# Adding the gated shift to x with an accumulating DMA instead of GpSimd additions

## The chip, the cores and the metric

The kernel runs on one core of a Trainium2 chip. The metric is the device time of one execution in microseconds. The kernel before took 761.77 us, the median of three runs (760.84 to 761.86). A profiled execution took 761.13 us; its span, from the first to the last recorded instruction, is 759.3 us. A core has five engines with queues of their own: TensorE (PE, matmuls), VectorE (DVE), ScalarE (ACT), GpSimd (POOL) and SyncE (SP, which here only issues DMAs). ACT and POOL can issue DMAs too.

## The reference

One transformer block with adaptive layer norms, on x of shape (8, 1024, 256) in float32; the eight batches are independent. Per batch there are six modulation rows sa, ca, ga, sb, cb, gb of 256 elements.

```python
h = _layernorm(x) * (1 + ca) + sa
x = x + ga * _L0_attn_ref(h, L0_attn_w_lhs, L0_attn_w_rhs)   # softmax((h*wl)(h*wr)^T) @ h
h = _layernorm(x) * (1 + cb) + sb
x = x + gb * _L0_ffn_ref(h, L0_ffn_W1, L0_ffn_b1, L0_ffn_W2, L0_ffn_b2)
```

The attention's values are h itself. With xn the normalized x, h = xn * (1 + ca) + sa, and since each row of the softmax sums to one, ga * attention = softmax @ (xn * (1 + ca) * ga) + sa * ga. The kernel uses this: it multiplies xn by the row (1 + ca) * ga, and adds the row sa * ga, the gated shift, to x ahead of the attention. That second addition is what the change is about.

## The kernel before, in words

A batch is 8 tiles of 128 rows, in two halves of 4 tiles (`g` = 0 and 1). x of a half is one tile in SBUF, 128 partitions x 4 x 256, in a pool of six buffers; it is loaded by ACT's DMA queue (`load_x`), updated in place and stored by SP's queue (`y_out`).

The main loop runs over batches `b` and row tiles `i`, and overlaps three things: the attention of batch b, the MLP of batch b - 1 and the preparation of batch b + 1. PE computes scores (`direct`, L410), the products with the normalized x (`product`, L499, and `pair_begin`/`pair_end`, L547 and L591, which do the same for two tiles with fewer multiplications), and the MLP (`pair_products`, L724, and `y_first`/`y_second`, L804). The fewer multiplications cost additions: POOL makes sums of weight blocks, of the exponentials (`left_sum`, `left_sums`, L563 to L575), of the MLP's input (`ffn_turn`, `hs`, L712 to L715), of its hidden layer (`pair_last` L778, `pair_turn` L797 to L800) and of the normalized x (`right_sums`, L532), and it adds the MLP's output to x (`y_add`, L878).

Transposes are made in three steps: DVE turns blocks of 32 x 32, four DMAs on SP's queue write the result to DRAM (`D_a`, `D_m`, `D_f`, `D_y`; L304), and one reads it back in the other order (L307; `X_a`, `X_f`, `Y`, `sc`). For the MLP's input the chain is: the second norm on ACT (`ffn_norm`, X_f), DVE's turn, D_f, X_f, then `hT` on DVE and ACT (L703, L705), then `hs` on POOL, then PE's L724.

For a half of the next batch, DVE takes statistics, ACT normalizes (L279, `xg`), DVE turns `xg` (`T_a`), and then `x_plus` and `xg_times` add the shift row to x and multiply `xg` by its row. Both rows lie broadcast in an SBUF tile `rows`, loaded per batch from a DRAM tile `rows_d` (`load_rows`).

The order of every engine's instructions is that of the program text: the function `pin` fixes it. `x_plus` and `xg_times` don't issue where they are called. They append to a queue, four entries each (one per tile), and calls of `spare` take one entry at a time. For the first half the calls are at i = 2 and the entries issue at i = 2 and 3; for the second half the calls are at i = 4 and the entries issue at i = 6 and 7, since the tiles i = 4 and 5 call no `spare`. In the first half POOL's order is: hs of the earlier half, 4 `x_plus`, 4 `xg_times`, the left sums for the pair of tiles 3 and 4. In the second: the left sums of the pair 6 and 7, 4 `x_plus`, 3 `xg_times`, `hs`, the fourth `xg_times`, `right_sums`. A half of x with the shift added is next read when the attention's result is added to it, in the next batch (`product_out` L513, `pair_out` L619, on DVE).

Of the kernel before, what the change touches and what calls it, by code (L numbers as in the profile page):

```python
# [13 lines left out]
ALU = mybir.AluOpType  # L14
# [3 lines left out]
P = 128  # L18
# [6 lines left out]
def adaln_block_kernel(  # L25
# [13 lines left out]
    nc = tc.nc  # L39
    B, S, D = x.shape  # L40
# [5 lines left out]
    TH = HALF // P  # L46
# [35 lines left out]
    x_t = {}  # L82
# [19 lines left out]
    def load_x0(q, queue):  # L102
# [11 lines left out]
        out=wv[ND : 2 * ND, :], in_=w_rhs.rearrange("a b (k p) -> (a b k) p", p=P)  # L114
# [518 lines left out]
    queue = deque()  # L633
# [5 lines left out]
    def later(out, in0, row, op):  # L639
        queue.append(lambda: nc.gpsimd.tensor_tensor(out, in0, row, op))  # L640
# [25 lines left out]

    def x_plus(b, g):

        for t in range(g * TH, (g + 1) * TH):
            xr = x_tile(b, t)  # L670
            later(xr, xr, rows_t[b][:, 1, :], ALU.add)
# [308 lines left out]
    rows_d = dram.tile([B, 4, D], F32, name="rows_d")  # L980
# [76 lines left out]
    for g in range(2):  # L1057
        x_plus(0, g)
# [18 lines left out]
    def early(b, i):  # L1077

        if b == 0:

            if i in (1, 3):
                prepare_rstd(1, i // 2)
            elif i == 5:
                ffn_rstd(0, 0)
            if i in (2, 3):
                prepare_norm(1, i - 2)
                x_plus(1, i - 2)
            if i in (3, 4):
                xg_times(1, i - 3)
            elif i == 5:  # L1090
                prepare_turn(1, 0)
                sum_w2()
            elif i == 6:
                load_x(2, 0)
        else:
            if i == 2 and b + 1 < B:
                prepare_norm(b + 1, 0)
            elif i == 6 and b + 2 < B:
                load_x(b + 2, 0)
# [22 lines left out]
    def norms(b, i):  # L1122
        if b > 0 and i == 0:
            ffn_blocks(b - 1, 1)
        if b == 0:
            if i == 0:
                prepare_start(1)
                prepare_stats(1, 0)
            elif i == 1:
                prepare_stats(1, 1, range(TH // 2))  # L1130
                sum_w1()
            elif i == 2:
                prepare_stats(1, 1, range(TH // 2, TH))
        elif b + 1 < B:
            if i == 1:
                prepare_start(b + 1)
                prepare_stats(b + 1, 0)
            elif i == 2:
                prepare_blocks(b + 1, 0)
                x_plus(b + 1, 0)  # L1140
                xg_times(b + 1, 0)
        elif i == 5:

            ffn_blocks(b, 0)
        if b == B - 1:
            return
        if i == 6:
            if b == 0:
                ffn_norm(b, 0)
            ffn_blocks(b, 0)  # L1150
# [234 lines left out]
    b = B - 1  # L1385
# [74 lines left out]
```

## Time and profile before

| What | us | Share |
|---|---|---|
| Median of three runs | 761.77 | |
| Profiled execution | 761.13 | |
| Its span | 759.3 | |
| PE busy, 3876 matmuls | 750.9 | 99% |
| DVE busy | 576.0 | 76% |
| POOL busy, 658 instructions | 570.8 | 75% |
| ACT busy | 374.7 | 49% |
| POOL, `x<-x,rows`, 64 additions | 44.8 | 6% |
| DMA queues, busy share of 16 engines | | 38.5% (SP), 3.6% (ACT) |

Busy time of an engine is the sum of its recorded instructions. Matmuls are pipelined, so two of them overlap in the records and PE's share says only that there is hardly a moment without one. A wait line names the instruction that was late, what released it, the total, how often, and the longest. In a timeline a line has the start, the length, the engine, the line of the kernel, what it writes and reads, and in brackets the idle time before it with what ended that. "SPq" is SP's queue issuing a DMA: its length is the issuing alone. Packets of a DMA are recorded too, with their queue, size and time.

### The profile page before, as it was taken

The page shows a single profiled execution, that of the slowest core. Times are in us where ns is not written, and L with a number is a line of the kernel's source. Part 1 is how long each engine was busy: PE and PEld are TensorE (multiplying, and loading weights), DVE is VectorE, ACT ScalarE, POOL GpSimd, SP SyncE. Part 2 cuts the span into 40 slices and gives each one's busy share as a digit, 9 for nine tenths or more (in the row PEclk, how much of TensorE's full clock was granted, in tenths as well). Part 3 has the DMA queues.
Part 4 walks back from the last instruction along what each step waited for, and adds up shares of the span by engine and source line. Part 5 has one row for each costly group of instructions (what it writes and reads, how often), then busy time and mean ns, then how long its engine had stood idle before and what let it go on. Part 6 is the DMA issues. An engine that isn't in the chain of part 4 may idle for free.

```text
span 759.3 us, 11880 instructions
## 1 busy us (share of the span) xinstructions
PE 750.9 (99%) x3876; PEld 623.3 (82%) x3876; DVE 576.0 (76%) x1259; ACT 374.7 (49%) x688; POOL 570.8 (75%) x658
## 2 busy tenths in 40 slices
PE   8999999999999999999999999999999999999998
PEld 4676789888897889878888888988889788888887
DVE  6787788778797788968888787877889677685632
ACT  3454545635466363655537444563546635252521
POOL 3542988788968799687887799777996888669731
PEclk9999999999999999999999999999999999999999
DMA  5314442465433554535534545235553354134220
GB/s 196 126 56 132 119 133 73 129 187 170 129 98 110 180 148 126 144 106 160 164 89 138 152 151 156 80 116 176 157 155 76 115 177 137 45 91 125 82 85 28
DMA packets 106213, 95.21 MB, mean 125 GB/s; under 512 B 29700, under 2 KB 98848, under 8 KB 106152
## 3 DMA queue, kind: packets, MB, share of 16 engines
q1 hardware_dynamic: 98408, 85.81, 38.5%
q10 hardware_dynamic: 7744, 8.65, 3.6%
q8 instruction: 30, 0.49, 0.3%
q14 instruction: 31, 0.25, 0.1%
HBM read 50.62 MB, written 43.81 MB: 124 GB/s over the span
## 4 chain that ended last, share of the span: by engine, by line
PE 88%; DVE 4%; ACT 2%; DMA 2%; POOL 2%; issue 1%; SPq 0%; DVEq 0%
PE psc L410 15%; PE pa L724 10%; PE pr L591 7%; PE po L499 6%; PE pb L724 6%; PE yc L804 6%; PE pc L724 6%; PE ya L804 6%; PE yb L804 6%; PE pq L591 5%; PE pp L547 5%; PE py L914 4%; PE yd L804 3%; DMA X_a<-D_a 1%; PE pmr L192 1%
## 5 line engine op out<-in xcount | busy, mean ns | idle before, releaser
L410 PE MATMUL psc<-rT,lT 128*128 128x512 f32 (+3 forms) x384 | 135.2, 487 | 1.0 <-ACT rT L373 0.8
L778 POOL TENSOR_TENSOR f<-f,kept 128x512 f32<-128x512 f32 x64 | 81.5, 1274 | 40.4 <-DVE f L777 18.5
L417 ACT COPY sc<-psc 128x512 f32<-128x512 f32 (+3 forms) x96 | 44.8, 475 | 120.4 <-PE psc L410 113.1
L482 ACT ACTIVATE pT<-pT 128x1024 f32<-128x1024 f32 x64 | 67.6, 1056 | 66.8 <-DVE pT L473 66.8
L410 PEld LDWEIGHTS psc<-rT,lT 128*128 128x128 f32 x384 | 66.3, 191 | 38.7 <-issue 24.1
L473 DVE TENSOR_TENSOR pT<-sc,pm 128x1024 f32<-128x1024 f32 x64 | 77.4, 1209 | 25.7 <-PE pm L466 15.3
L499 PE MATMUL po<-xg,pT 128*128 128x257 f32 x352 | 80.7, 380 | 0.0
L461 DVE TENSOR_REDUCE m<-sc 128x1 f32<-128x1024 f32 x64 | 77.4, 1209 | 1.3 <-ACT sc L417 1.0
L499 PEld LDWEIGHTS po<-xg,pT 128*128 128x128 f32 x352 | 66.2, 190 | 10.0 <-issue 1.0
L745 ACT COPY kept<-pa 128x512 f32<-128x512 f32 x64 | 37.3, 583 | 68.6 <-PE pa L724 68.6
L724 PE MATMUL pb<-hs,w1s 128*128 128x256 f32 x256 | 65.9, 380 | 0.1
L724 PE MATMUL pc<-hT,w 128*128 128x256 f32 x256 | 65.7, 379 | 0.0
L640 POOL TENSOR_TENSOR x<-x,rows 128x256 f32<-128x256 f32 x64 | 44.8, 732 | 24.9 <-ACT xg L279 10.7
L787 ACT ACTIVATE f<-f 128x512 f32<-128x512 f32 x64 | 39.8, 622 | 35.9 <-POOL f L778 35.9
L878 POOL TENSOR_TENSOR x<-x,Y 128x512 f32<-128x512 f32 x28 | 35.1, 1276 | 29.4 <-DMA Y<-D_y 23.9
L724 PEld LDWEIGHTS pb<-hs,w1s 128*128 128x128 f32 x256 | 48.5, 190 | 7.3 <-DVE f L763 0.8
L724 PEld LDWEIGHTS pc<-hT,w 128*128 128x128 f32 x256 | 48.6, 190 | 6.7
L804 PE MATMUL yc<-f,w2s 128*128 128x256 f32 x224 | 51.3, 379 | 0.0
L433 DVE STREAM_TRANSPOSE Tm<-sc 128x896 f32<-128x896 f32 (+6 forms) x49 | 34.4, 702 | 19.9 <-ACT sc L417 19.1
L804 PEld LDWEIGHTS yc<-f,w2s 128*128 128x128 f32 x224 | 41.5, 190 | 8.1 <-issue 2.9
L797 POOL TENSOR_TENSOR ft<-f 128x256 f32<-128x256 f32 x56 | 40.9, 730 | 7.6 <-ACT f L788 7.5
L547 PEld LDWEIGHTS pp<-xg,pT 128*128 128x128 f32 x336 | 41.9, 192 | 5.1 <-issue 1.4
(164 smaller groups left out, 1823.3 us busy)
## 6 DMA issues: line engine op xcount, KB each, us to landing
D_f<-T_f SPq DMA_DIRECT2D x60, 128.0 KB, 2.4
X_f<-D_f SPq DMA_DIRECT2D x15, 512.0 KB, 3.9
D_a<-T_a SPq DMA_DIRECT2D x56, 128.0 KB, 3.4
D_y<-T_y SPq DMA_DIRECT2D x56, 128.0 KB, 2.7
Y<-D_y SPq DMA_DIRECT2D x14, 512.0 KB, 3.4
out_dram<-x SPq DMA_DIRECT2D x14, 512.0 KB, 4.2
X_a<-D_a SPq DMA_DIRECT2D x13, 512.0 KB, 3.4
x<-in_L_attn_x_dram ACTq DMA_DIRECT2D x12, 512.0 KB, 3.9
```

What stands on the lines that cost most here:

```text
L410: nc.tensor.matmul(psc[:, : hi - lo], lhsT=lT_t[b, i // TH][:, k, ts(i % TH, P)], rhs=rT_t[b, n][:, k, lo - n * HALF : HALF], start=(k == ...
L417: nc.scalar.copy(score_row(b, i)[:, lo // V : hi // V, :], psc[:, : hi - lo].rearrange("p (n v) -> p n v", v=V),)
L461: nc.vector.tensor_reduce(m, score_row(b, i), AX.XY, ALU.max)
L473: nc.vector.tensor_tensor(pT.rearrange("p j (a v) -> p j a v", v=V), score_columns(b, i), pm[:, :P].rearrange("p (j a v) -> p j a v", j=1, ...
L482: nc.scalar.activation(pT_t[b, i], pT_t[b, i], AF.Exp)
L499: nc.tensor.matmul(po[:, : D + 1], lhsT=pT[:, t, :], rhs=xg_t[b][:, t, 0 : D + 1], start=(t == 0), stop=(t == NT - 1),)
L547: nc.tensor.matmul(out, lhsT=lhs[:, t, :], rhs=xg_t[b][:, h * TH + t, P : P + XS], start=(t == 0), stop=(t == TH - 1),)
L591: nc.tensor.matmul(out, lhsT=lhs[:, t, :], rhs=rhs[:, t, :], start=(t == 0), stop=(t == TH - 1),)
L640: queue.append(lambda: nc.gpsimd.tensor_tensor(out, in0, row, op))
L724: nc.tensor.matmul(out, lhsT=lhsT, rhs=rhs, start=True, stop=True)
L778: nc.gpsimd.tensor_tensor(f[:, c::NH, hi], f[:, c::NH, hi], kept[:, None, hi].to_broadcast([P, 2, H2]), ALU.add,)
L804: nc.tensor.matmul(out, lhsT=lhs(c), rhs=rhs(c), start=(c == 0), stop=(c == NH - 1))
```

## The change

In batches 2 to 7 `x_plus` appends one entry instead of four. The entry issues a DMA from POOL's queue, which reads the shift row of `rows_d` in DRAM, broadcast to 128 partitions and 4 tiles, and adds it to x of the half where it lies (`accum_op`). Batches 0 and 1 keep POOL's additions. That makes 12 DMAs of 512 KB in place of 48 additions of 128 x 256. `xg_times` is as before, with its four entries.

```diff
     def x_plus(b, g):
 
+        if b > 1:
+            queue.append(lambda: nc.gpsimd.dma_start(
+                out=x_t[b, g],
+                in_=rows_d[b][1:2, :].partition_broadcast(P).to_broadcast([P, TH, D]),
+                accum_op=ALU.add,
+            ))
+            return
         for t in range(g * TH, (g + 1) * TH):
             xr = x_tile(b, t)
             later(xr, xr, rows_t[b][:, 1, :], ALU.add)
```

The instructions of PE, DVE, ACT and SP stay the same and in the same order. On POOL the DMA stands where the first of the four additions stood; since three entries are gone, the entries of `xg_times` are taken three calls earlier, and in the second half all four now come before `hs`. The instructions that read x next (L513 and L619 on DVE, L656 on ACT, the store on SP) get a wait for the DMA's landing; six waits of PE for POOL, in L499, go away.

## The prediction

> **What bounds the kernel now.** First the page: busy time by engine, then the chain that ended last.
>
> ```profile
> PE 750.9 (99%) x3876; PEld 623.3 (82%) x3876; DVE 576.0 (76%) x1259; ACT 374.7 (49%) x688; POOL 570.8 (75%) x658
> PE 88%; DVE 4%; ACT 2%; DMA 2%; POOL 2%; issue 1%; SPq 0%; DVEq 0%
> ```
>
> PE is busy 99% of the span and carries 88% of the chain; POOL, from which the change takes work, has 2%. Busy time of pipelined matmuls can hide stalls, so I looked for a rhythm: the chain in order of time has one run of 16 `yc` matmuls in the second half of each batch from the second on.
>
> ```profile
> 114.80 3.46 PE yc L804 x16
> ...
> 205.23 3.46 PE yc L804 x16
> ...
> 295.66 3.46 PE yc L804 x16
> ...
> 386.26 3.46 PE yc L804 x16
> ...
> 476.69 3.46 PE yc L804 x16
> ...
> 567.12 3.46 PE yc L804 x16
> ...
> 658.06 3.45 PE yc L804 x16
> ```
>
> The steps are 90.43, 90.43, 90.60, 90.43, 90.43 and 90.94 us. Four are equal to the hundredth: in these PE issues back to back. The other two lose 0.17 and 0.51 us. All 12 new DMAs lie between 114 and 620 us, so a lighter POOL can return at most 0.17 + 0.51 = 0.68 us, or 0.09%. The larger of the two (at 595 us) isn't POOL's: there the scores wait for ACT's `rT`, which waits for the landing of `X_a`. So the question is not what is gained but whether one of the twelve sites gets late enough to stop PE.
>
> The timeline of POOL in the third batch (b = 2), first half's additions:
>
> ```profile
> 203.03 2.84 POOL L640 TENSOR_TENSOR x<-x,rows 128x256 f32<-128x256 f32 x4
> 205.83 2.78 POOL L640 TENSOR_TENSOR xg<-xg,rows 128x256 f32<-128x256 f32 x4
> ...
> 216.70 1.27 POOL L778 TENSOR_TENSOR f<-f,kept 128x512 f32<-128x512 f32 x1 [2.82 <-DVE rs L275]
> ```
>
> Second half's additions, and what comes after them:
>
> ```profile
> 246.57 2.77 POOL L640 TENSOR_TENSOR x<-x,rows 128x256 f32<-128x256 f32 x4
> 249.31 2.11 POOL L640 TENSOR_TENSOR xg<-xg,rows 128x256 f32<-128x256 f32 x3
> 255.37 0.73 POOL L712 TENSOR_TENSOR hs<-hT 128x256 f32<-128x256 f32 x1 [3.95 <-DVE hT L703]
> ...
> 256.73 0.73 POOL L714 TENSOR_TENSOR hs<-hT,hs 128x256 f32<-128x256 f32 x1
> ```
>
> Both runs end in an idle time of POOL, 2.82 and 3.95 us, that waits for another engine: shortening the run lengthens the idle, and PE sees nothing. Then the DMA queue of SP, ACT and PE around the second site:
>
> ```profile
> 246.24 1.83 SPq L304 DMA_DIRECT2D D_f<-T_f  x4
> 250.49 0.34 SPq L307 DMA_DIRECT2D X_f<-D_f  x1
> ```
>
> ```profile
> 254.48 0.81 ACT L705 ACTIVATE hT<-X_f,modT 128x512 f32<-128x512 f32 x1 [0.37 <-DMA X_f<-D_f]
> ```
>
> ```profile
> 259.82 0.59 PE L724 MATMUL pa<-hs,w 128*128 128x256 f32 x2
> 260.25 1.03 PE L724 MATMUL pb<-hs,w1s 128*128 128x256 f32 x4
> ```
>
> The MLP's input is turned through DRAM just there: D_f, X_f, then `hT`, then `hs` on POOL, then PE. `hs[1]` (L714) ends at 257.46 and PE wants it at 260.25: 2.79 us of slack. In the six batches that issue the new DMA (b = 1 to 6) the same difference is 2.79, 2.79, 2.38, 2.30, 1.48 and 2.72.
>
> **What the skill says.** The Trainium skill, "DMA: Bandwidth & Descriptors", section "SWDGE vs HWDGE vs iDMA": accumulating in a DMA exists only for DMAs issued from GpSimd, where Q7 cores compute the descriptors in software. The kernel before issues none from POOL (its queues are `hardware_dynamic` and `instruction`), so the trace neither confirms nor prices this. "Perfetto Trace Analysis", section "DMA Instruction — SWDGE (GPSIMD)": cores 0 and 1 generate, and the recorded end is their last descriptor, not the landing; no run here shows it yet. "GPSIMD Engine Reference", section 3.1, gives about 2.6 cycles an element for a two-input add: 256 x 2.6 / 1.2 GHz = 555 ns plus dispatch, and the trace agrees with 732 ns for 256 columns.
>
> **The change part by part.** *Removed*: 48 of the 64 `x<-x,rows` additions (b = 2 to 7, 8 each): 48 x 0.732 = 35.1 us of POOL, 6% of its busy time. PE gets none of it, by the idles above: 0.
>
> *Added on POOL*: 12 DMA issues, one per half, each with 128 x 4 destination rows of 1 KB, so 512 writes, and two reads for each (the row of `rows_d` and the old x), 1024. Let X be how long POOL is held. Lower end 1 us: the DMA page's specification table has about 1 us to the first byte on this path. Upper end 14.2 us: its fit has a fixed 2.0 us for a DMA, and its 1 MiB example has 144 descriptors a side; were all 2.0 us generation, that is 13.9 ns each, times 1024. The page lays most of the 2.0 us on the receipt, and only 1.0 - 0.6 = 0.4 us apart from the hardware path: 2.8 ns each. My value is 1 + 1024 x 0.0028 = 3.9 us (an estimate).
>
> What X may be for nothing: at the first site, the 2.84 us removed plus the idle, which in the six batches is 2.29 to 2.82: 5.1 to 5.7 us. Beyond it `f+kept` (L778) is late, then ACT's relu (0.7 us of slack, 217.97 to 218.64), behind it on ACT an exponent and the copy `kept`, whose release PE awaits at 224.88 (copy ends 224.17): 0.7 us more. PE stops from about 7 us. The left sums (L563 to L575), queued behind the DMA too, end 7 us before PE's use (213.88 against 220.84). At the second site: 2.78 + idle (2.72 to 5.20) - 0.73 for the fourth `xg` multiplication, which now comes before `hs`, + the slack of `hs`: 7.5 to 9.5 us. With X = 3.9 both are covered: 0. Without the cover it would be 12 x (3.9 - 2.8) = 13 us.
>
> *Moved*: x_plus puts one entry in the queue instead of four, so `xg` comes three pops earlier and PE loses one wait on POOL per batch; the transposes that read `xg` before it is overwritten end at 200.3 for the first half and 220.1 for the second (DVE's timeline), before either site: 0. SP's and ACT's queues keep their order.
>
> *Added waits*: the next reader of x on DVE (L513, L619), ACT (L656) and SP's output now also wait for the landing. Issued at about 203, the half is first read by L513 after PE's `po` of 265.70, 62 us later, the second half still later; the slowest landing of 512 KB here is 6.8 us. Cost 0.
>
> *Added traffic*: the load of x, also 512 KB in packets of 1 KB (512 packets, 241.87 to 244.12 us), has a mean of 54 ns a packet: 32 packets on each of 16 engines, 1.7 us. "Collectives: The Full Stack", section "The bandwidth ceiling", says an accumulating copy needs two source reads and runs at half the rate of a copy: 108 ns, 3.5 us of every engine. Lower end 1.7 (only as costly as a copy); upper end 200 ns a packet, what the 4 KB packets of X_f take here, 6.4 us. At the first site the turn X_a <- D_a is beside it, whose reader on ACT comes at 219.68, 11 us after its landing: 0. At the second, D_f and X_f are beside it. They share the engines, so X_f lands later by about half to all of 3.5 us: 1.7 to 3.5. Against the slacks, 1.7 costs 0.2 (b = 5 alone), 3.0 costs 0.2+0.2+0.6+0.7+1.5+0.3 = 3.5, 4.0 costs 9.5 us. I take 2.0: 0.5 us in b = 5; less some 0.2 that POOL's relief may return at the two uneven steps.
>
> *Sum*: the profiled execution took 761.13 us, 759.3 span + 1.83 around it. 761.13 + 0.5 - 0.2 = 761.4. It stood 0.64 under the median 761.77, so against the median: about 762.0.
>
> **Rivals.** (1) *Issue too long*: POOL held over 7 us at the first sites. For it: software descriptors, 512 rows with two reads, and nothing in the trace to say they are cheap. Against it: the page's "small, variable". At X = 8: six first sites x 1 us plus about 1 = 7, so 769; at 10: 6 x 3 + 9 = 27, so 789. This is the slower side, and it decides at X about 7. (2) *Traffic*: X_f late beyond 2.5 us at the second site. For it: DMA share 0.63 in 246 to 252 us. Against it: D_f starts before the issue ends. At 3 to 4 us of lateness 765 to 771. (3) *The relief counts*: the 0.68 us come back whole, 761.1; 0.2% (1.5 us) would need stalls that the rhythm excludes. (4) *The addition leaves POOL in name only*: POOL is held until the data lands. A load of 512 KB lands 3.9 us after its issue; with 1.7 us more for the second read X is near 5.6, still under 7: 762 as well, with the two idles used up.
>
> **How the numbers follow.** Hidden (with 3 and 4): 0.58. Rival 1: 0.22. Rival 2: 0.15. Faster by more than 0.2%, from something unseen: 0.05. A fifth of a per cent, 1.5 us, is about what measurement tells (the runs spread over 1.0 us). So faster 0.05, same 0.58, slower 0.37. The likeliest case alone: 761.0 to 763.3. The range: 760.3 below (0.05 left out) and 775 above (X to about 8.7, lateness to 4.6; about 0.13 left out).
>
> **What would show it.** Right: `yc` still 90.4 us apart, PE's waits on POOL absent, POOL's busy time near 536 us with the idle before L778 and L712 there in part. Wrong: idle before L778 gone and ACT's relu waiting on POOL (rival 1); a longer wait of `hT` for X_f and PE idle at `pa` or `pb` (rival 2); DVE's L513 or L619 waiting for the accumulating DMA (landing price wrong).

## The result, and the profile after

The changed kernel takes 789.24 us (median of four runs, 787.4 to 791.13) against 761.46 us for the kernel before on the same chip: ratio 1.0364, 95% interval 1.034 to 1.0387. It is 28 us slower; 762.0 was forecast, in a range up to 775. The side was a rival's, the second one (traffic at the second site); its size was not foreseen.

The page of the changed kernel, busy time, DMA queues and chain:

```profile
PE 762.3 (97%) x3876; PEld 624.9 (80%) x3876; DVE 580.5 (74%) x1259; ACT 373.5 (48%) x688; POOL 553.6 (70%) x622
...
q1 hardware_dynamic: 98408, 85.81, 36.9%
q0 software_dynamic: 6336, 6.29, 7.6%
...
PE 69%; DMA 15%; DVE 5%; POOL 3%; ACT 3%; issue 2%; SPq 2%; DVEq 0%; POOLq 0%
```

POOL lost work as intended (the twelve issues, 1.3 us each, give back 15.6 of the 35.1 us removed). But DMA now carries 15% of the chain (2% before), and PE's busy time rose by 11 us with the same 3876 matmuls. The run of `yc` matmuls, 90.43 us apart before, now starts at 115.11, 209.90, 304.71, 398.62, 493.70, 591.03 and 684.61 us: steps of 94.79, 94.81, 93.91, 95.08, 97.33 and 93.58, together 26.2 us more than before. So the loss lies in the six batches that issue the DMAs. PE's own waits, largest three:

```profile
PE pa L731 <- DVE hT L710: 8.0, 6, 2.8
PE pb L731 <- POOL hs L721: 3.5, 6, 0.7
PE pa L731 <- ACT kept L752: 2.5, 3, 1.4
```

Six waits for `hT`, six for `hs`: one per batch, at the second site. The timeline there (third batch, lines of POOL, SP, ACT and PE picked out):

```profile
250.90 1.82 SPq L304 DMA_DIRECT2D D_f<-T_f  x4
...
251.60 1.30 POOL L670 DMA_DIRECT2D x<-rows_d  x1
...
256.13 0.34 SPq L307 DMA_DIRECT2D X_f<-D_f  x1
256.51 4.24 SPq L304 DMA_DIRECT2D D_m<-Tm  x4
...
264.79 0.81 ACT L712 ACTIVATE hT<-X_f,modT 128x512 f32<-128x512 f32 x1 [6.01 <-DMA X_f<-D_f]
...
265.33 0.70 PE L731 MATMUL pa<-hT,w 128*128 128x256 f32 x2 [1.12 <-DVE hT L710]
```

POOL is held 1.3 us and is not the problem. X_f is issued at 256.13 and `hT` starts at 264.79: 8.7 us, where the kernel before took 4.0 (250.49 to 254.48). The new DMA's own group:

```profile
L670 POOL DMA_DIRECT2D x<-rows_d x12: 1292/1298/1438, 113.3 to 634.2; - x12
...
DMA to landing us min/median/max: 9.5/10.5/11.7
```

It lands 10.5 us after its issue. The busy stretches of two microseconds have the DMA engines' share and GB/s at the end:

```profile
252.00:254.00 2.00, 2.00 (x12) 1.72 (x11) 1.23 (x2) 0.50 (x1) 2.00 (x4) 1.00 1.03 331
254.00:256.00 2.00, 2.00 (x11) 1.77 (x10) 2.00 (x2) 0.99 (x1) 1.71 (x3) 1.00 0.84 122
256.00:258.00 2.00, 2.00 (x15) 1.87 (x14) 1.60 (x5) 0.81 (x3) 0.00 (x0) 1.00 1.15 76
258.00:260.00 2.00, 2.00 (x20) 2.00 (x19) 1.42 (x2) 0.78 (x2) 0.00 (x0) 1.00 1.05 69
260.00:262.00 2.00, 2.00 (x18) 1.95 (x17) 0.00 (x0) 0.00 (x0) 0.00 (x0) 1.00 1.06 172
```

From 256 to 260 us the DMA engines are recorded as fully occupied (1.15 and 1.05) and move 69 to 76 GB/s, less than a quarter of the 331 a moment earlier. In the packet records these are 62 to 76 packets of 1 KB of the new queue per microsecond. No packet of SP's queue starts between 255.7 and 260.1: X_f, asked for at 256.13, hasn't begun. In the kernel before, its first packet starts 0.97 us after its issue; here it is 2.9 to 5.6 us in five of the six batches, after 260 to 375 packets of the new queue. So POOL is not late, and the bytes are few: one slow transfer is under way, and what is behind it waits.

In the remaining one (b = 5) it is D_f that is held:

```profile
536.61 3.44 SPq L304 DMA_DIRECT2D D_f<-T_f  x4
546.19 0.34 SPq L307 DMA_DIRECT2D X_f<-D_f  x1
```

X_f is issued 9.6 us after D_f, against 4.7 before. D_f had begun when the DMA's packets came, and it isn't stopped: from 540 to 543 us, 83 to 110 packets of the new queue pass per microsecond and 56 to 79 of D_f between them; in the third batch 323 of D_f passed in one microsecond (253 to 254), just ahead of the new queue's.

Of the 26.2 us, 6.8 are not waiting at all. After the stalls of the batches b = 1, 2 and 5 the granted TensorE clock is half for 3.4, 3.4 and 6.8 us; half of these 13.65 us is lost. In the same view, with PE's granted clock third from the end:

```profile
268.00:270.00 2.00, 2.00 (x6) 1.61 (x6) 1.89 (x6) 0.33 (x2) 1.92 (x3) 0.51 0.94 319
```

PE counts as busy there and does half the work, which is where most of its 11 us more of busy time come from. Without the clock, the first `pb` matmul of the six second sites starts 2.84, 2.59, 2.09, 2.78, 4.26 and 2.32 us later after the `yd` matmuls than before, 16.9 us in all; the wait for `kept` grew by 1.8. Together with the clock this is 25.5 of the 26.2 us.

### The profile page after: what moved, and what is told of

Read it like the earlier page. It is cut to its first block, busy times and chain, and to the rows that moved or that the text cites. A ratio compares the mean times of both kernels' runs of the same rounds, so it can differ in the third digit from the quotient of the medians.

```text
span 785.9 us, 11892 instructions
## 1 busy us (share of the span) xinstructions
PE 762.3 (97%) x3876; PEld 624.9 (80%) x3876; DVE 580.5 (74%) x1259; ACT 373.5 (48%) x688; POOL 553.6 (70%) x622
## 4 chain that ended last, share of the span: by engine, by line
PE 69%; DMA 15%; DVE 5%; POOL 3%; ACT 3%; issue 2%; SPq 2%; DVEq 0%; POOLq 0%
PE psc L410 10%; PE pa L731 9%; PE pb L731 6%; PE pc L731 6%; DMA X_f<-D_f 6%; PE po L499 6%; PE pr L591 5%; PE ya L811 4%; PE yb L811 4%; PE pp L547 4%; PE py L921 4%; PE yc L811 4%; PE pq L591 3%; DMA D_f<-T_f 3%; DMA D_m<-Tm 2%
## 5 line engine op out<-in xcount | busy, mean ns | idle before, releaser
L499 PE MATMUL po<-xg,pT 128*128 128x257 f32 x352 | 80.7, 380 | 0.0
L499 PEld LDWEIGHTS po<-xg,pT 128*128 128x128 f32 x352 | 66.2, 190 | 10.0 <-issue 1.0
L731 PE MATMUL pb<-hs,w1s 128*128 128x256 f32 x256 | 69.0, 393 | 3.6 <-POOL hs L721 3.5
L731 PE MATMUL pc<-hT,w 128*128 128x256 f32 x256 | 68.1, 390 | 0.0
L719 POOL TENSOR_TENSOR hs<-hT 128x256 f32<-128x256 f32 x16 | 11.6, 725 | 71.5 <-DVE hT L710 71.5
L885 POOL TENSOR_TENSOR x<-x,Y 128x512 f32<-128x512 f32 x28 | 35.1, 1275 | 35.7 <-DMA Y<-D_y 35.7
L731 PEld LDWEIGHTS pb<-hs,w1s 128*128 128x128 f32 x256 | 48.8, 195 | 14.1 <-POOL hs L721 6.2
L731 PEld LDWEIGHTS pc<-hT,w 128*128 128x128 f32 x256 | 50.2, 197 | 7.7 <-DVE pr L609 0.4
L731 PE MATMUL pa<-hT,w 128*128 128x256 f32 x128 | 39.0, 387 | 8.0 <-DVE hT L710 8.0
```

The source lines that it names most:

```text
L499: nc.tensor.matmul(po[:, : D + 1], lhsT=pT[:, t, :], rhs=xg_t[b][:, t, 0 : D + 1], start=(t == 0), stop=(t == NT - 1),)
L731: nc.tensor.matmul(out, lhsT=lhsT, rhs=rhs, start=True, stop=True)
```

## The experiments

All comparisons are with the kernel before on the same chip.

**Which site?** The DMA for one half only; the other half keeps POOL's additions.

```diff
-        if b > 1:
+        if b > 1 and g == 0:      # first half only; g == 1: second half only
```

> The accumulating DMA only for the first half of x (6 DMAs), POOL's additions for the second half. Theory (the MLP's turn is held up): all of the loss comes from the second half's DMA, which holds up the read of X_f beside it; without it the time is that of the kernel before, 761 to 762 us, and ACT's hT follows the issue of X_f by 4.0 us as before. Rival (any such DMA costs, through POOL's issue or through the clock): half of the loss stays, about 775 us.

> The DMA only for the second half. Theory: the whole loss is here, 786 to 790 us, hT 8.7 to 9.6 us after the issue of X_f. Rival (any such DMA costs): about 775 us.

First half only: 763.09 us, ratio 1.003 (1.0017 to 1.0042). Second half only: 792.32 us, 1.0407 (1.0385 to 1.043). The whole loss is the second half's DMA. The first isn't quite free: 1.7 us, not the nothing that the theory said. POOL's left sums wait for ACT's exponentials 22.7 us in total (14 times) against 11.5 (8 times) before, and DVE's `pT` for the turn of the scores 8.5 us (7 times) against 5.9 (4 times). On PE the loss comes in steps of about 0.1 us at `pr` (L591), `pc` and `pb` (L731), where `pb` waits for DVE's `f` (L770); what makes that late was not followed further. In the run with the second half alone PE waits above all for one thing:

```profile
PE pa L731 <- DVE hT L710: 13.9, 6, 3.5
```

It loses somewhat more than forecast. In two of its six batches `hT` follows X_f's issue by 8.9 and 9.0 us, as expected; in the other four by 3.8 to 4.4, and D_f was held instead (10.2 to 12.4 us from D_f's issue to X_f's).

**Does the engines' unit of service matter?** The second half's DMA in four, one tile each.

```diff
+            def pieces(tiles=range(TH) if g else range(1)):
+                n = TH // len(tiles)
+                for j in tiles:
+                    nc.gpsimd.dma_start(
+                        out=x_t[b, g][:, ds(j * n, n), :],
+                        in_=rows_d[b][1:2, :].partition_broadcast(P).to_broadcast([P, n, D]),
+                        accum_op=ALU.add,
+                    )
```

> As the changed kernel, but the second half's DMA cut into four, one per tile, issued one after the other (POOL is held four times 1.3 us, 5.2 us, of the 6.7 us that were covered in the third batch). Theory A (an engine that has begun a DMA of this queue serves no other queue until its share of that DMA is done): the read of X_f gets in after one piece or two, hT follows its issue by 5 to 7 us instead of 9, and most of the loss goes: 764 to 775 us. Theory B (the engines are only shared, and it is the total time of the packets that delays X_f): the same bytes, the same delay, 786 to 792 us.

784.55 us, 1.0314 (1.0289 to 1.0338): 5 us better, short of both numbers, nearer to B. `hT` followed the issue of X_f by 8.9, 8.8, 7.3, 7.4, 4.0 and 6.5 us (where 4.0 stands, D_f had been held instead). The split is no clear gain: in the profiled executions the half clock costs 1.7 us where it cost 6.8 in the changed kernel, a difference as large as the 5 us. Theory A doesn't hold as it was put: in the changed kernel D_f's packets pass inside one DMA of the new queue (b = 5). So the next question was what makes the transfer so long.

**What is slow: the second read, or where the row is read?** The added row from the SBUF tile `rows`, which holds it already.

```diff
-                in_=rows_d[b][1:2, :].partition_broadcast(P).to_broadcast([P, TH, D]),
+                in_=rows_t[b][:, 1:2, :].to_broadcast([P, TH, D]),
```

> As the changed kernel, but the added row is read from the broadcast tile rows in SBUF and not from rows_d in DRAM. Theory C (the 512 reads of one DRAM row are what makes the packets slow, 110 to 219 ns in the mean): packets of 60 to 100 ns, landing in 5 to 6 us instead of 10.5, and 765 to 775 us. Theory D (the second read and the addition are what costs): packets within 10% of those before and 785 to 791 us.

766.36 us, 1.0075 (1.006 to 1.0091). 23 of the 28 us are gone, with the same 512 rows added by the same queue at the same places; 6.8 of them are the half clock, which this profile doesn't show after its start. The landing, and the engines while the transfer runs:

```profile
DMA to landing us min/median/max: 5.9/7.0/8.0
```

```profile
252.00:254.00 2.00, 2.00 (x17) 1.90 (x16) 1.49 (x5) 1.01 (x2) 0.00 (x0) 1.00 1.13 220
```

220 GB/s in place of 69 to 76, at the same occupancy; about half of it is X_f, which moves already, and the new queue passes 175 to 185 packets of 1 KB per microsecond where it passed 62 to 76. It is theory C in the time; the packets' mean fell only to 106 to 137 ns, not to 60 to 100, and the landing is 7.0 us in the median, not 5 to 6. Of the 5 us that remain, the first site has 1.5 (shown below), and at the second sites the first `pb` is late by 2.8 in all.

**One row, or DRAM at all? The addition, or the reading?** Two kernels that part these: one adds 512 different rows of DRAM (those of x), the other copies the one row without adding (so it leaves x out of the sum).

```diff
-                in_=rows_d[b][1:2, :].partition_broadcast(P).to_broadcast([P, TH, D]),
+                in_=x[b, ts(g, HALF), :].rearrange("(t p) d -> p t d", p=P),
```

```diff
-                accum_op=ALU.add,
```

> As the changed kernel, but the DMA adds the 512 rows of 1 KB of the input x itself from DRAM instead of 512 times one row (so the output is another; the bytes, packets, dependencies and the queue are the same). Theory E (the reads of one and the same DRAM row stand in line, about 14 ns each, and while they wait the engines serve no other queue): rows at 512 addresses are read at the pace seen with the source in SBUF, landing in 5 to 6 us, 764 to 770 us. Theory F (an accumulating DMA that reads DRAM is slow, whatever it reads): 786 to 792 us, landing near 10 us.

> The DMA of the changed kernel without the addition: the row is copied over x, 512 times from the same address (so x is left out of the sum and the output is another; places and waits are the same). Theory E (one row read 512 times is what takes the time): still 7 us or more from the first packet to the last, 775 to 790 us. Theory F (the accumulation is what costs): 2 to 3 us, as the load of x has, and 761 to 764 us.

Different rows: 767.09 us, 1.0076 (1.0061 to 1.0091), as with SBUF. One row without the addition: 790.92 us, 1.0383 (1.0349 to 1.0417), as the changed kernel and just over the 775 to 790 forecast. Their landings, first with different rows, then with the copy of one row:

```profile
DMA to landing us min/median/max: 5.5/7.5/9.2
```

```profile
L670 POOL DMA_DIRECT2D x<-rows_d x12: 789/789/957, 112.8 to 633.4; - x12
...
DMA to landing us min/median/max: 8.6/9.2/10.3
```

Different rows land later than the 5 to 6 us expected, but the time falls as theory E said. The two runs settle the cause of the 23 us: it is not the addition, nor the software queue's descriptors, nor DRAM as such, but the 512 reads of one 1 KB row of DRAM.

**Does POOL's queue have precedence?** The same copy of one row, issued from ACT's queue.

```diff
-            queue.append(lambda: nc.gpsimd.dma_start(
+            queue.append(lambda: nc.scalar.dma_start(
```

> The plain copy of the row over x, 512 reads of one DRAM row (x is left out of the sum), issued from ACT's queue instead of POOL's; it starts some 6 us earlier than in the changed kernel in the second half, before the turn of the MLP's input. Theory E (it is the reading of one row that takes the time and holds the others up, whatever queue asks): 6 us or more from the first packet to the last, almost no packet of SP's queue between, and 775 to 795 us. Rival G (POOL's queue is served ahead of the others): SP's packets go on between, 762 to 770 us.

792.9 us, 1.041 (1.038 to 1.044). The same slowness from another queue:

```profile
L670 ACTq DMA_DIRECT2D x<-rows_d x12: 366/377/387, 107.6 to 632.4; - x12
...
DMA to landing us min/median/max: 8.4/8.9/10.1
```

At its second site in the third batch, SP's queue has just issued D_m, and the read-back waits for it:

```profile
245.67 1.76 SPq L304 DMA_DIRECT2D D_m<-Tm  x4
...
257.12 0.54 SPq L307 DMA_DIRECT2D sc<-D_m  x1
```

In the packet records half of D_m's 512 packets pass before 248 us and the other half after 252; between, 60 to 103 packets of ACT's queue pass per microsecond and none of SP's. So it is not a precedence of POOL's queue. The engines are far from occupied in these four microseconds, 0.34 and 0.22:

```profile
248.00:250.00 2.00, 2.00 (x11) 1.66 (x10) 0.92 (x3) 1.43 (x3) 1.92 (x2) 1.00 0.34 88
250.00:252.00 2.00, 2.00 (x7) 1.12 (x6) 1.83 (x4) 0.48 (x1) 1.92 (x3) 1.00 0.22 65
```

The busy share of the DMA engines thus doesn't tell whether another queue gets through.

**Fewer, longer reads.** The row laid four times side by side in DRAM, so that a partition reads 4 KB once.

```diff
+    rows_w = dram.tile([B, TH * D], F32, name="rows_w")
+    for j in range(TH):
+        nc.sync.dma_start(out=rows_w[:, ts(j, D)], in_=rows_sb[:, 1, :])
...
-                out=x_t[b, g],
-                in_=rows_d[b][1:2, :].partition_broadcast(P).to_broadcast([P, TH, D]),
+                out=x_t[b, g].rearrange("p t d -> p (t d)"),
+                in_=rows_w[b].partition_broadcast(P),
```

> As the changed kernel, but the row is first laid four times side by side in DRAM (4 KB a batch, written once at the start by four small DMAs on SP's queue, up to 1 us later start), so that a partition is one read of 4 KB: 128 reads in place of 512. Theory E with a cost per read: 128 x 14 ns, below 4 us from first to last, 763 to 770 us. Rival (the cost is by bytes of one region of DRAM): near 8 us and 785 to 790 us.

774.66 us, 1.0173 (1.015 to 1.0196). The transfer became short, 3.9 us in the median from first packet to last (8.0 in the changed kernel), as theory E says; the time missed the expected 763 to 770. In four of the six batches D_f was held (D_f to X_f 8.0 to 8.7 us, against 4.3 to 4.8 before), in the run from SBUF in three. The first `pb` of the second sites is late by 6.4 us in all, against 2.8 in the run from SBUF. Why the whole loss is 8 us greater than there, though the transfer is no longer, was not separated.

**What the shorter transfer costs, and whether a place for it exists.** First the first half alone, from SBUF; then both moved to stretches where the profile of before shows the DMA engines idle; then the second half alone moved; then both moved, with the row from DRAM again. `x_plus_now` issues the DMA where it is called.

```diff
             elif i == 3:
                 left_sums(b, i)
+                x_plus_now(b + 1, 0)
...
+                if i == 5:
+                    x_plus_now(b + 1, 1)
                 pair_turn(c)
```

> The DMA for the first half only, with the row read from the tile rows in SBUF; POOL's additions for the second half. Theory: the first site has slack for a transfer of 4 to 5 us, so the 1.7 us that were lost with the row read from DRAM go and the time is that of the kernel before, 761 to 762 us. Rival (any transfer there delays the turn through X_a): about 763 us, as with the row in DRAM.

> Both DMAs, with the row read from SBUF, issued at places where the profile of before shows the DMA engines idle and POOL waiting: the first half's after the left sums of tiles 3 and 4 (engines nearly idle from 209 to 216 us of the third batch), the second half's in tile 5 between the last f+kept and the sums ft (engines idle from 232 to 239 us, POOL idle 1.5 us). Theory (only a collision with a turn through DRAM costs): the time of the kernel before, 761 to 762.5 us, and hT 3.8 to 4.1 us after the issue of X_f. Rival (the issue on POOL or any such traffic costs wherever it stands): 764 us or more.

> The second half's DMA alone, from SBUF, in tile 5 as in the run with both moved; POOL's additions for the first half. Theory: 760.8 to 762 us, no difference from the kernel before. Rival: the issue of 1.3 us on POOL makes the sums ft late, whose slack is about 1.4 us there: 763 us or more.

> As the run with both DMAs moved, but with the row read from DRAM as in the changed kernel. Theory (place and length of the transfer decide together): 7 to 8 us of transfer outlast the idle stretch of the second place by 1 to 3 us and meet the turn of the scores there, far less than the 28 us of the changed kernel: 763 to 770 us. Rival (reading one row from DRAM costs the same anywhere): 785 us or more.

| Run | us | Ratio (95%) |
|---|---|---|
| first half, SBUF | 762.86 | 1.0019 (1.0012 to 1.0026) |
| both moved, SBUF | 764.37 | 1.0038 (1.0026 to 1.0051) |
| second half moved, SBUF | 761.37 | 1.0003 (0.9994 to 1.0011) |
| both moved, DRAM row | 787.81 | 1.0347 (1.0321 to 1.0372) |

The first half from SBUF loses 1.5 us, as the rival said: reading the row from SBUF doesn't help at that site, so its loss is not that of the one row. The second half's place is right: in the run with it alone the time is that of the kernel before. POOL issues it just where the kernel before has it idle 1.5 us:

```profile
232.76 1.27 POOL L788 TENSOR_TENSOR f<-f,kept 128x512 f32<-128x512 f32 x1
233.97 1.29 POOL L669 DMA_DIRECT2D x<-rows  x1
235.29 0.74 POOL L807 TENSOR_TENSOR ft<-f 128x256 f32<-128x256 f32 x1
```

With both moved the time is the rival's too (764 or more). The first half's place, after the left sums, was badly chosen. It is quiet itself, but the turn of the normalized x (D_a, X_a) follows, on which PE's next scores wait. PE's waits for that turn's reader, in the run with both moved from SBUF, and in the one from DRAM:

```profile
PE psc L410 <- ACT rT L340: 2.5, 4, 1.0
```

```profile
PE psc L410 <- ACT rT L340: 15.2, 6, 4.4
```

Against my 763 to 770, the DRAM row costs 27 us at these places too. It is the rival's number, but not at the same place: X_f is no longer held (`hT` 3.8 to 4.0 us after its issue in all six batches), the scores are. At both places tried, a transfer of 7 to 8 us found some turn to hold up.

The transfers side by side, from the packet records (first packet to last, median of the DMAs in the kernel):

| Kernel | What is read | First to last, us | Time, us |
|---|---|---|---|
| changed | one DRAM row, 512 times, added | 8.0 | 789.2 |
| copy, POOL | one DRAM row, 512 times | 7.2 | 790.9 |
| different rows | 512 DRAM rows, added | 4.3 | 767.1 |
| from SBUF | SBUF row of each partition, added | 4.5 | 766.4 |
| from SBUF, both moved | SBUF row of each partition, added | 3.3 | 764.4 |
| wide | 4 KB of DRAM, 128 times, added | 3.9 | 774.7 |

## Why the prediction was wrong

**What bounds the kernel**: right. The even steps of `yc` said that nothing could be gained and that only a late site could cost; no run was faster than the kernel before, and the best, 1.0003, is no different.

**Removed, moved, added waits**: right at nothing, as far as the runs show. No wait for the landing shows in the trace; it comes 10.5 us after the issue, some 60 us ahead of the reader.

**Added on POOL**: X was put at 3.9 us, between 1 and 14.2. It is 1.3 us for the addition in 512 packets, and 0.79 for the plain copy in 128. So rival 1 had no ground. The Trainium skill's "small, variable" ("DMA: Bandwidth & Descriptors", section "Anatomy of one DMA") was the better guide, as this trace shows; my upper bound was of no use.

**Added traffic**: this is the step that failed. I priced a packet by the load of x, 54 ns, doubled for the second read, had 3.5 us for the transfer and X_f late by 1.7 to 3.5 us. The doubling was right: no packet of an accumulating DMA with 1 KB rows is below 101 ns, and from SBUF, undisturbed, the transfer takes 3.3 us. But from one DRAM row it lasts 8.0, since the load of x reads 512 different rows and so was the wrong thing to price by. The row to look at stood in the same trace: the load of `rows`, which reads one row of 2 KB 128 times. Its packets run from 180.00 to 181.84 us in the third batch; for the microsecond from 180 us, in which no packet of SP's starts, the view shows:

```profile
180.00:181.00 1.00, 1.00 (x5) 0.50 (x4) 0.96 (x4) 0.62 (x3) 0.92 (x2) 1.00 0.61 166
```

The 128 reads take 1.84 us, or 14.4 ns each. Times 512 that is 7.4 us, against 8.0 measured. The second half of the same step failed too: the engines were taken to be shared, so that X_f would be late by half to all of the transfer's time. X_f's whole reading, or D_f's, stood behind most of it, and `hT` was 5.0 to 6.1 us late. The first site, put at nothing, cost 1.5 to 1.7 us, whether the row came from DRAM or SBUF; through which term isn't known.

**The slack behind it**: right. `hT` now starts 8.25, 8.00, 7.50, 8.20, 9.66 and 7.73 us after the start of the last `yd` matmul of its batch, where it started 2.62, 2.35, 2.55, 2.73, 3.54 and 2.74 after it: 5.6, 5.7, 5.0, 5.5, 6.1 and 5.0 us late. Less the slacks of the prediction (2.79, 2.79, 2.38, 2.30, 1.48, 2.72) that leaves 18.4 us of stall; PE's own matmuls show 16.9. Without the clock, which the prediction didn't have, its own working with these latenesses gives 761.1 + 18.4 + 0.6 = 780. The other 6.8 us are the half clock.

**Rival 2** named the mechanism and the line in which it would show, and was given 0.15. Its argument against, that D_f starts before the issue ends, says nothing of X_f, which is behind the transfer, and doesn't save D_f either, which had begun in b = 5 and was slowed all the same.

**Left open**: whether the DMA engines themselves hold the other queue's packets back, or the DRAM that both use. One thing speaks for the engines: with the row from SBUF, where the transfer touches no DRAM, 273 and 352 of its packets still pass before X_f's first where that is late, as many as in the changed kernel. But no run was made to part the two, and why X_f is stopped while D_f is only slowed isn't known. Nor do the runs part the number of reads from the number of times that one place in DRAM is read, which are the same in all of them.

Which stall costs the clock follows a pattern in the traces. The half-clock stretches of one run begin a whole number of steps of 3.413 us apart: at 172.45, 268.02 and 551.33 us in the changed kernel, 28 and 111 steps. In the step just before each of these, PE was idle for 1.63, 1.50 and 2.78 us by its recorded matmuls. In no step of the other three batches was it idle for more than 1.43 us; a stall there fell short or across two steps. Over all kernels, each of the 14 steps from 100 to 740 us with over 1.9 us of idle PE was followed by half clock, none under 1.5, and 4 of the 11 between. So whether a stall of 2 us costs the clock depends also on where it falls among these steps; why some half-clock stretches last two steps isn't known.

## What to carry to other kernels

A DMA that broadcasts one row of 1 or 2 KB from DRAM was paid here by the number of reads of that row, not by bytes. Price such a DMA by a transfer in the profile that does the same, and where the row is in SBUF already, broadcast from there. A DMA whose result nobody waits for can still stop or slow the transfers beside it, so find what is issued in the time it lasts, and what slack that has. Where the bottleneck engine issues back to back, taking work from another engine can hardly gain and may cost.

## What the runs showed that was not expected

Reads of one DRAM row pass at about 14 to 16 ns each (1.84 us for 128, 7.2 us and 8.0 us for 512), with or without an addition, and from ACT's queue as slowly as from POOL's (landing in 8.9 and 9.2 us). Packets of SP's queue either cease meanwhile for about 4 us or pass slowly between the slow ones; the recorded occupancy of the DMA engines was over 1 in the one case and 0.2 to 0.4 in the run from ACT's queue, so it doesn't show who is held. An addition in the DMA took at least 101 ns for 1 KB, about twice the 54 ns in the mean of a copy. After PE had been idle 1.5 us or more within one 3.4 us step, the granted clock was half for 3.4 to 6.8 us in three of six batches, which added 6.8 us to the waiting.
